# A selective-scan hybrid block on one core: the step's softplus cut into groups, and other places and allowances for the work between the scans

## The chip, the core and the metric

The kernel runs on one core of a Trainium2 chip. The metric is device time in microseconds, the median of the runs. The engines are TensorE (PE; PEld is its weight load), VectorE (DVE), ScalarE (ACT), GpSimd (POOL) and SyncE (SP), whose queue issues all DMAs here.

## What is computed

The input x has 8 images of 64x64 positions and 96 channels, all float32. Two layers follow each other.

```python
# layer 0, on group-normalized x; per image, L = 4096 positions, 192 inner channels, 16 states, 4 directions
xz = x @ in_proj_w.T;  xh, z = split(xz)
xc = silu(conv3x3_depthwise(xh) + conv_b)
xs = [xc[diag], xc[anti], reversed(xc[diag]), reversed(xc[anti])]
dts, Bs, Cs = split(x_proj(xs))
delta = softplus(dt_proj(dts) + bias)
h = h * exp(delta * A) + (delta * u) * B        # a recurrence over the 4096 positions, for each of 16 states
y = sum over states (h * C) + D * u
out = (layernorm(y of the four directions, put back) * ln_w + ln_b) * silu(z) @ out_proj_w.T
x = x + out
# layer 1: linear attention (no softmax) on layernorm(x), then a feed-forward net with values rounded to fp8
```

## The kernel before

**Steps and states.** The recurrence is the core of the work. The diagonal and the antidiagonal order lie in one tile together (2 x 64 partitions by 3 groups of channels), so an image is walked twice: q = 0 forward, q = 1 backward. Each walk is cut into 8 steps of 512 positions, so an image has 16 steps and the program 128. A step m has 16 states n, and the main loop of `run` runs over all 2048 pairs i = 16 m + n. A tile of a step holds 128 partitions x 3 groups x 512 positions.

**What a state takes.** Work of several states is in flight at once; at loop index i:

- ACT makes decay(i+2) = exp(a * delta), three activations of 512 (L923), and, where the state is of kind "A", `times_b(i+2)`: eight activations of 192 that multiply the transposed delta*u by B (feedT, L937).
- VectorE does `recur(i)`: three scans of 512 (L958). The scan reads its feed from one of three PSUM banks. Where the state is of kind "D", VectorE first makes the feed itself with three products (L962) from a row that TensorE has spread (L947).
- TensorE does `turn(i+1)`: for an "A" state, it transposes feedT into the three feed banks (L945), each as soon as the scan of state i has left it. Between these it does `reduce(i-LAG)`: it transposes h of an earlier state into the sum y (L993).
- POOL does `keep(i-1)` (the last column of h as carry for the next step, L974) and `read(i-1)`: h times C (L979).
- SP fetches row C for state i+4 (L914).

The kinds are set by `FEED = "DADADADADADAAAAA"`: six "D" states and ten "A" states to a step. LAG is 4, and h has six buffers, decay three, feedT two.

**The prologue of a step** makes what its states need: rows of dt, B and C (L835, L840, L845, L848), softplus, and delta*u with its transposed copy. The softplus is computed as max(v, 0) + ln(1 + e) with e = exp(-|v|), and a correction for the rounding of 1 + e: ACT does Abs by groups (L860), then one Exp (L862) and one Ln (L865) over all 1536 columns; POOL does two scalar operations (L869, L870) and two products of tiles (L872, L874); VectorE adds max(v, 0) group by group (L879); POOL makes du = delta * u (L886); TensorE and ACT transpose it (L891, L893). The prologue of step m + 2 starts at state 13 of step m.

**Everything else** (the statistics and convolution of the next image: `measures`, `front`; the norms, attention and feed-forward net of the previous image: `tail`) is written as generators. Each yields, ahead of each piece, the engine it is for, a rough cost in us, how many loop indices it must wait (by the table LAGS, or by a number of its own) and whether it needs a PSUM bank; two banks are free for this. The class `Work` hands them out: the main loop calls `work.at(engine, place)` once per index for ACT (between decay and feedT), VectorE (between the second and the third scan) and POOL (after `read`), and three times for TensorE (after each third of turn and reduce). Each call adds an allowance (PLACES: gain and most) to the engine's credit, and pieces are taken while the credit is positive; urgent ones (prologues) may overdraw it. Engines work in the order in which instructions stand, so a piece that waits holds up all behind it on its engine. `work.finish` hands out everything at once until a condition holds; it is called at state 4 + 1 of an image for all that is left (`all_done`), and in `bring` when the next step's input is not there yet.

Of the kernel before, what the change touches and what calls it, by code (L numbers as in the profile page):

```python
# [67 lines left out]
def weights(tc, const, w):  # L68
# [125 lines left out]

LAGS = {
    "AV": (1, 0), "AP": (0, 1), "AG": (0, 0), "VA": (1, 0), "VP": (0, 1), "VG": (0, 0), "PA": (1, 0), "PV": (1, 0),
    "PG": (1, 0), "GA": (1, 0), "GV": (1, 0), "GP": (1, 1), "SA": (3, 0), "SV": (3, 0), "SP": (3, 0), "SG": (3, 0),
# [27 lines left out]
class Work:  # L225
# [4 lines left out]
    PLACES = {"A": (2.0, 2.5), "V": (1.5, 2.0), "G": (3.5, 5.0), "P": (0.85, 1.2), "S": (9.0, 9.0)}  # L230

    def __init__(self, banks):
        self.now = 0
        self.alone = False
        self.urgent, self.jobs, self.streams = [], [], []
        self.free = [(b, -9) for b in banks]
        self.long = []
        self.credit = dict.fromkeys(self.PLACES, 0.0)

    def start(self, gen, urgent=False):  # L240
        j = SimpleNamespace(gen=gen, tag="S", us=0.0, bank=False, spin=False, ready=(self.now, 0), done=False)
        self.proceed(j, None, 0)
        (self.urgent if urgent else self.jobs).append(j)
        return j

    def proceed(self, j, given, place):
# [6 lines left out]
        its, late = LAGS.get(last + tag, (0, 0))  # L253
        if lag is not None:
            its, late = abs(lag), 0
        j.tag, j.us, j.bank, j.spin = tag, us, needs, lag == -1
        j.ready = (self.now + its, 2 if late else 0) if its or late else (self.now, 0)

    def bank_for(self, j, place):
        if j not in self.urgent and not self.alone:  # L260
            if any(u.tag == "P" and u.bank for u in self.urgent) or j.bank == "long" and self.long:
                return None
        for i, (b, when) in enumerate(self.free):
            if when < self.now or place == 2 or self.alone:
# [12 lines left out]
    def at(self, tag, place=0):  # L277
        gain, most = self.PLACES[tag]
        self.credit[tag] = min(most, self.credit[tag] + gain)
        for j in self.urgent + self.jobs:  # L280
            while not j.done and j.tag == tag:
                if j.ready > (self.now, place) and (j.spin or not self.alone):
                    break
                if not self.alone:
                    if self.credit[tag] <= (0.0 if j not in self.urgent else -1.5 if tag == "P" else -99.0):
# [40 lines left out]
    def finish(self, enough):  # L326
# [7 lines left out]
        self.credit = dict.fromkeys(self.PLACES, 0.0)  # L334
# [224 lines left out]
def tail(tc, work, x, out, k, at, b):  # L559
# [3 lines left out]
    with tc.tile_pool(name=f"t1_{b}", bufs=1, **area) as p1:  # L563
# [3 lines left out]
        with tc.tile_pool(name=f"t2_{b}", bufs=2, **area) as p2:  # L567
# [3 lines left out]
            def join(c):  # L571
                s = slice(4 * c, 4 * c + 4)

                def tile(name, shape, bufs=2):
# [11 lines left out]
                while c >= 2 and c - 2 not in joined:  # L586
                    yield SPIN
                gate = tile("gate", [HC, 2, CH])
                nc.sync.dma_start(out=gate, in_=at.gate[:, :, c * CH : (c + 1) * CH])
                st, mv = tile("st", [P, 4, 6]), tile("mv", [P, 4, 2])  # L590
                yn = ys[0]
                for j in range(2):
# [12 lines left out]
                    yield dve(1.0, 0)  # L605
# [3 lines left out]
                    work.release(ps)  # L609
                r, m = yield from rsqrt(nc, p2, k, mv, P, 4, "n")  # L610
# [3 lines left out]
                yg = tile("yg", [HC, 2, CH])  # L614
# [27 lines left out]
                yield dve(1.7, 0)  # L642
# [38 lines left out]
        def attention():  # L681
# [14 lines left out]
            kf = yield from small([DM, DM], "kf", vk, k.w_ff)  # L696
# [11 lines left out]
        with tc.tile_pool(name=f"t3_{b}", bufs=3, **area) as p2:  # L708

            def layers(c):  # L710
# [22 lines left out]
                yield dve(1.7, 0)  # L733
# [48 lines left out]
def run(tc, pool, psum, dram, x, out, w, NB):  # L782
# [37 lines left out]
    def prologue(m):  # L820
# [8 lines left out]
        ps = yield bank(1.0, 0)  # L829
        v = view(ps, P, TB, NX)  # L830
        for j in range(TB):
            if j == 2:
                yield pe(0.8)
# [5 lines left out]
        rows = o.rows = tile("rows", [P, TB, NX])  # L839
# [14 lines left out]

        e = tile("e", [P, G, T], 1)
        for g in range(G):
# [5 lines left out]
        nc.scalar.activation(e, e, AF.Exp, scale=-1.0)  # L862
        yield act(1.5, 1)
        delta = tile("delta", [P, G, T])
        nc.scalar.activation(delta, e, AF.Ln, bias=w.one)  # L865
        duT = tile("duT", [P, TB * G, P])
        f = duT.rearrange("p (g k) t -> p g (k t)", g=G)
        yield gp(3.0)
        nc.gpsimd.tensor_scalar(f, e, 1.0, 1.0, ALU.mult, ALU.add)  # L869
        nc.gpsimd.tensor_scalar(f, f, -1.0, 1.0, ALU.add, ALU.mult)  # L870
        yield gp(3.4, 1)
        nc.gpsimd.tensor_tensor(e, e, f, ALU.subtract)  # L872
        yield gp(3.4, 1)
        nc.gpsimd.tensor_tensor(delta, delta, e, ALU.add)  # L874
        for g in range(G):
# [5 lines left out]
        o.delta = delta  # L881
        yield gp(3.4)
        while m and not made[m - 1].multiplied:
            yield "G", 0.0, -1, False
        du = o.du = tile("du", [P, G, T], 1)
        nc.gpsimd.tensor_tensor(du, delta, u, ALU.mult)  # L886
        for j in range(G):
            ps = yield bank(0.45)
            for i in range(4):
                r, g = divmod(4 * j + i, G)  # L890
                nc.tensor.transpose(ps[:, i * P : (i + 1) * P], du[:, g, r * P : (r + 1) * P], w.ident)  # L891
# [3 lines left out]
        o.duT = duT  # L895

    def bring(m):
# [4 lines left out]
        made[m] = SimpleNamespace(u=u, c={}, multiplied=False)  # L902
# [22 lines left out]
    def times_b(i):  # L925

        m, n = divmod(i, NS)
        o = made[m]
        if FEED[n] == "D":
            return  # L930
# [18 lines left out]
    def recur(i):  # L949
        m, n = divmod(i, NS)  # L950
        _, q, _ = steps[m]
        h = hs[i] = pool.tile([P, G, T], F32, tag="h", name=f"h_{i}", bufs=6)
# [10 lines left out]
        if n == FEED.rindex("D"):  # L963
            made[m].multiplied = True
        scan(0)
        scan(1)
        work.at("V")
# [13 lines left out]
    def reduce(i, part):  # L981
# [15 lines left out]
        if q and n in (1, 2, 3) and part == 2:  # L997
            for j in range(4 * (n - 1), 4 * n):
# [4 lines left out]
                )  # L1003
        if q and n in (8, 9, 10) and part == 2:
# [4 lines left out]
            )  # L1009
        if part == 2:  # L1010
# [35 lines left out]

    def between(b):
# [20 lines left out]
    work.start(prologue(0), urgent=True)  # L1068
    work.finish(lambda: not work.urgent)
# [135 lines left out]
```

## Time and profile before

| what | us |
|---|---|
| median of 3 runs (12140.42 to 12148.66) | 12146.02 |
| the profiled execution | 12157.04 |
| its span | 12155.1 |
| start of the first scan, end of the last | 445.9, 11772.6 |
| POOL busy with L979 | 7073.1 |
| VectorE busy with L958, both forms | 6500.6 + 883.9 |
| ACT busy with decay L923, with feedT L937 | 3976.8, 3670.8 |
| POOL busy with L872, L874, L886 | 441.9, 441.0, 449.4 |
| ACT busy with Exp L862, with Ln L865 | 190.2, 199.9 |
| mean granted TensorE clock | 0.909 of full |

A row of the groups names line, engine, operation, output and inputs with their shapes and the count; then follow the total busy time, the mean of one in ns, and the idle time of the engine just before these instructions with what ended it. A row of the waits names who waited, for whom, the total in us, how often, and the longest. A row of a timeline has start, length, engine, line, operation and count, and in brackets the idle time before it.

### The profile page before, as it was taken

The page shows a single profiled execution, that of the slowest core. Times are in us where ns is not written, and L with a number is a line of the kernel's source. Part 1 is how long each engine was busy: PE and PEld are TensorE (multiplying, and loading weights), DVE is VectorE, ACT ScalarE, POOL GpSimd, SP SyncE. Part 2 cuts the span into 40 slices and gives each one's busy share as a digit, 9 for nine tenths or more (in the row PEclk, how much of TensorE's full clock was granted, in tenths as well). Part 3 has the DMA queues.
Part 4 walks back from the last instruction along what each step waited for, and adds up shares of the span by engine and source line. Part 5 has one row for each costly group of instructions (what it writes and reads, how often), then busy time and mean ns, then how long its engine had stood idle before and what let it go on. Part 6 is the DMA issues. An engine that isn't in the chain of part 4 may idle for free.

```text
span 12155.1 us, 187007 instructions
## 1 busy us (share of the span) xinstructions
PE 9958.7 (82%) x62804; PEld 8012.1 (66%) x62804; DVE 9683.1 (80%) x11092; ACT 9501.2 (78%) x19842; POOL 9737.6 (80%) x6927
## 2 busy tenths in 40 slices
PE   4698889888898888988888888988889888888874
PEld 3476667666676666766677666766667666666653
DVE  1488998878888888888888888888888878888971
ACT  1588888877888788877888878887788878878862
POOL 0588998878988788888888889888898888889972
PEclk9799999998998989989899999999989899988985
DMA  2334333533335433353333433344333443322331
GB/s 53 91 92 124 100 93 94 136 104 96 94 88 134 112 94 93 90 141 101 95 90 106 127 102 95 90 127 117 92 92 93 132 108 93 100 87 84 100 93 42
DMA packets 1138471, 1213.47 MB, mean 100 GB/s; under 512 B 464998, under 2 KB 744167, under 8 KB 1137511
## 3 DMA queue, kind: packets, MB, share of 16 engines
q1 hardware_dynamic: 1137510, 1201.51, 36.0%
q8 instruction: 499, 8.18, 0.3%
q14 instruction: 462, 3.78, 0.1%
HBM read 877.94 MB, written 323.09 MB: 99 GB/s over the span
## 4 chain that ended last, share of the span: by engine, by line
PE 29%; ACT 22%; DVE 20%; POOL 11%; issue 9%; SPq 4%; DMA 4%; DVEq 0%; POOLq 0%; ACTq 0%
DVE h L958 13%; ACT feedT L937 8%; PE y L993 7%; PE feed L945 7%; ACT decay L923 6%; POOL h L979 6%; DVE feed L962 4%; PE bank L493 3%; DMA cc<-crow 2%; PE bank L835 2%; SPq L538 2%; PE bank L877 1%; POOL delta L874 1%; PE feed L947 1%; PE bank L858 1%
## 5 line engine op out<-in xcount | busy, mean ns | idle before, releaser
L979 POOL TENSOR_TENSOR h<-h,cc 128x1536 f32<-128x1536 f32 x2048 | 7073.1, 3454 | 401.7 <-DMA cc<-crow 205.0
L958 DVE TENSOR_TENSOR_SCAN h<-decay,carry,feed 128x512 f32<-128x512 f32 x5376 | 6500.6, 1261 | 623.0 <-PE feed L945 510.4
L923 ACT ACTIVATE decay<-delta,a_neg 128x512 f32<-128x512 f32 x6144 | 3976.8, 713 | 1303.6 <-DVE h L958 1298.1
L945 PE MATMUL feed<-ident,feedT 128*128 128x128 f32 x15360 | 2738.5, 303 | 1508.3 <-DVE h L958 1237.9
L993 PE MATMUL y<-ident,h 128*128 128x128 f32 x24576 | 3804.4, 289 | 68.6 <-ACT ys L1021 37.3
L937 ACT ACTIVATE feedT<-duT,rows 128x192 f32<-128x192 f32 x10240 | 3670.8, 443 | 1.6 <-PE feed L945 1.1
L993 PEld LDWEIGHTS y<-ident,h 128*128 128x128 f32 x24576 | 3154.2, 151 | 527.5 <-issue 483.4
L945 PEld LDWEIGHTS feed<-ident,feedT 128*128 128x128 f32 x15360 | 1970.4, 155 | 2118.5 <-DVE h L958 667.9
L962 DVE TENSOR_TENSOR feed<-feed,du 128x512 f32<-128x512 f32 x2304 | 1442.5, 687 | 210.7 <-PE feed L947 205.8
L974 POOL COPY carry<-h 128x3 f32<-128x3 f32 x2048 | 395.4, 193 | 1065.4 <-DVE h L958 985.8
L958 DVE TENSOR_TENSOR_SCAN h<-decay,feed 128x512 f32<-128x512 f32 x768 | 883.9, 1202 | 102.5 <-PE feed L945 83.2
L493 PE MATMUL bank<-wf,xp 97*128 97x192 f32 x4320 | 873.6, 334 | 1.7 <-ACT xp L458 1.7
L947 PE MATMUL feed<-x,pick 77*128 77x512 f32 x1536 | 846.4, 633 | 0.7
L493 PEld LDWEIGHTS bank<-wf,xp 97*128 97x128 f32 x4320 | 704.8, 195 | 28.8 <-issue 15.9
L879 DVE SCALAR_TENSOR_TENSOR delta<-bank,delta 128x512 f32<-128x512 f32 x381 | 258.5, 678 | 287.0 <-POOL delta L874 159.6
L886 POOL TENSOR_TENSOR du<-delta,u 128x1536 f32<-128x1536 f32 x128 | 449.4, 3511 | 10.6 <-DVE delta L879 10.6
L877 PE MATMUL bank<-x,ws 13*128 13x512 f32 x762 | 439.4, 657 | 20.8 <-DVE delta L879 20.8
L872 POOL TENSOR_TENSOR e<-e,duT 128x1536 f32<-128x1536 f32 x128 | 441.9, 3452 | 16.7 <-ACT delta L865 16.6
L858 PE MATMUL bank<-x,ws 13*128 13x512 f32 x766 | 436.6, 650 | 17.3 <-ACT x L848 17.3
L874 POOL TENSOR_TENSOR delta<-delta,e 128x1536 f32<-128x1536 f32 x128 | 441.0, 3446 | 0.1
L947 PEld LDWEIGHTS feed<-x,pick 77*128 77x128 f32 x1536 | 261.0, 201 | 152.7 <-issue 96.2
L835 PE MATMUL bank<-wx,u 128*128 128x77 f32 x3048 | 356.5, 273 | 0.0
(260 smaller groups left out, 8885.1 us busy)
## 6 DMA issues: line engine op xcount, KB each, us to landing
cc<-crow SPq DMA_DIRECT2D x4096, 128.0 KB
u<-seq SPq DMA_DIRECT2D x256, 384.0 KB
wide<-ys SPq DMA_DIRECT2D x512, 192.0 KB
ut<-image SPq DMA_DIRECT2D x768, 64.0 KB
seq<-us SPq DMA_DIRECT2D x128, 384.0 KB
part<-ys SPq DMA_DIRECT2D x64, 768.0 KB
y<-part SPq DMA_DIRECT2D x64, 768.0 KB
y<-wide SPq DMA_DIRECT2D x256, 192.0 KB
```

The costliest lines, as they stand in the source:

```text
L493: nc.tensor.matmul(v[:, j, :], flat[:, o : o + P], k.wf[:, i, :], start=(i == 0), stop=(i == 8), skip_group_check=True)
L835: nc.tensor.matmul(v[:, j, :], u[:, g, j * P : (j + 1) * P], w.wx[:, q, g, :], start=(g == 0), stop=(g == G - 1))
L874: nc.gpsimd.tensor_tensor(delta, delta, e, ALU.add)
L877: nc.tensor.matmul(ps, w.ws[:, q, g, :], x[0 : 2 * NR + 1, :], start=True, stop=True)
L923: nc.scalar.activation(decays[i][:, g, :], made[m].delta[:, g, :], AF.Exp, scale=w.a_neg[:, q, g, n : n + 1])
L937: nc.scalar.activation(f[part], o.duT[part], AF.Copy, scale=scale)
L945: nc.tensor.transpose(feed[g][:, j * P : (j + 1) * P], feeds[i][:, j * G + g, :], w.ident)
L947: nc.tensor.matmul(feed[0], w.pick[:, FEED[:n].count("D"), :], made[m].x, start=True, stop=True)
L958: nc.vector.tensor_tensor_scan(h[:, g, back], a[:, g, back], feed[g][:, back], init, ALU.mult, ALU.add)
L962: nc.vector.tensor_tensor(feed[g], feed[0], made[m].du[:, g, :], ALU.mult)
L979: nc.gpsimd.tensor_tensor(hs[i], hs[i], c.unsqueeze(1).to_broadcast([P, G, T]), ALU.mult)
L993: nc.tensor.matmul(y[:, j, :], hs[i][:, g, r * P : (r + 1) * P], w.ident, is_transpose=True, start=(n == 0 and j % 4 == 0), stop=(n == NS ...
```

## The change

- **Softplus by groups.** The prologue ends after dt, B and C. It then starts three generators `group(g)`, each with 512 columns: Abs and Exp (one piece), Ln, two scalar operations and two products on POOL, VectorE's correction, and POOL's du. When all three are through, three generators `turned(j)` transpose du. du gets two buffers instead of one, `rows` three instead of two. The groups of step m wait until those of m - 1 are corrected and the last feedT of m - 2 is made. The prologue starts at state 9 instead of 13, and its first matmuls come in four pieces instead of two.
- **Allowances by kind.** Each engine has two gains, one for a "D" and one for an "A" state: ACT 1.45 and 0.3 (for state i + 2), VectorE 0.3 and 1.9, TensorE 1.0 and 0.9, POOL 2.0 and 2.0. Urgent pieces may overdraw only to -1.0 (ACT) or -0.4. TensorE's extra matmuls of `reduce` are counted as spent.
- **Places.** VectorE's place is behind the third scan, after TensorE's. ACT has a second place at the end of the index, behind feedT. LAGS names the place at which the piece before was handed out.
- **Ends may run over.** The fronts and tails of all images are one stream, `windows`, which may go on into the next image's steps; the `finish` at an image's start is gone. `hurry` hands out urgent pieces at once where the next decay or feedT needs them.
- **Buffers.** LAG is 3 instead of 4, h has five buffers instead of six, the tail's first pool has three instead of two (gate and yg stay at two). In `join`, the wait for c - 2 and the fetch of gate come after the first sums; its and `layers`' bn_stats take their lag from LAGS.
- **Start.** The prologues of steps 0 and 1 are handed out together before the loop.

```diff
-    PLACES = {"A": (2.0, 2.5), "V": (1.5, 2.0), "G": (3.5, 5.0), "P": (0.85, 1.2), "S": (9.0, 9.0)}
+    GAIN = {"A": (1.45, 0.3), "V": (0.3, 1.9), "G": (2.0, 2.0), "P": (1.0, 0.9), "S": (9.0, 9.0)}
+    MOST = {"A": 3.2, "V": 2.2, "G": 2.5, "P": 1.2, "S": 9.0}
...
-    def at(self, tag, place=0):
-        gain, most = self.PLACES[tag]
-        self.credit[tag] = min(most, self.credit[tag] + gain)
-        for j in self.urgent + self.jobs:
+    def at(self, tag, place=0, kind="D"):
+        self.credit[tag] = min(self.MOST[tag], self.credit[tag] + self.GAIN[tag][kind != "D"])
+        for j in self.urgent + ([] if self.hurried else self.jobs):
...
-                    if self.credit[tag] <= (0.0 if j not in self.urgent else -1.5 if tag == "P" else -99.0):
+                    if self.credit[tag] <= (0.0 if j not in self.urgent else -1.0 if tag == "A" else -0.4):
...
-        for g in range(G):
-            ps = yield bank(0.85)
-            nc.tensor.matmul(ps, w.ws[:, q, g, :], x[0 : 2 * NR + 1, :], start=True, stop=True)
-            yield act(0.6)
-            nc.scalar.activation(e[:, g, :], ps, AF.Abs)
-            work.release(ps)
-        nc.scalar.activation(e, e, AF.Exp, scale=-1.0)
-        yield act(1.5, 1)
-        delta = tile("delta", [P, G, T])
-        nc.scalar.activation(delta, e, AF.Ln, bias=w.one)
...
+        def group(g):
+
+            ps = yield bank(0.85)
+            nc.tensor.matmul(ps, w.ws[:, q, g, :], x[0 : 2 * NR + 1, :], start=True, stop=True)
+            yield act(0.6)
+            nc.scalar.activation(e[:, g, :], ps, AF.Abs)
+            work.release(ps)
+            nc.scalar.activation(e[:, g, :], e[:, g, :], AF.Exp, scale=-1.0)
+            yield act(1.2)
+            nc.scalar.activation(delta[:, g, :], e[:, g, :], AF.Ln, bias=w.one)
+            yield gp(1.05)
+            nc.gpsimd.tensor_scalar(f[:, g], e[:, g], 1.0, 1.0, ALU.mult, ALU.add)
+            nc.gpsimd.tensor_scalar(f[:, g], f[:, g], -1.0, 1.0, ALU.add, ALU.mult)
+            yield gp(1.15)
+            nc.gpsimd.tensor_tensor(e[:, g], e[:, g], f[:, g], ALU.subtract)
+            yield gp(1.15)
+            nc.gpsimd.tensor_tensor(delta[:, g], delta[:, g], e[:, g], ALU.add)
+            ps = yield bank(0.85)
+            nc.tensor.matmul(ps, w.ws[:, q, g, :], x[0 : 2 * NR + 1, :], start=True, stop=True)
+            yield dve(0.7)
+            nc.vector.scalar_tensor_tensor(delta[:, g, :], ps, 0.0, delta[:, g, :], ALU.max, ALU.add)
+            work.release(ps)
...
+            yield gp(1.15)
+            nc.gpsimd.tensor_tensor(o.du[:, g], delta[:, g], u[:, g], ALU.mult)
...
-        h = hs[i] = pool.tile([P, G, T], F32, tag="h", name=f"h_{i}", bufs=6)
+        h = hs[i] = pool.tile([P, G, T], F32, tag="h", name=f"h_{i}", bufs=5)
...
         scan(0)
         scan(1)
-        work.at("V")
         scan(2)
...
-    LAG = 4
+    LAG = 3
...
             if at == LAG + 1:
-                work.finish(all_done)
-                work.stream(between(b))
+                begun[0] = b
+                if b == 0:
+                    work.stream(windows())
...
         if i + 2 < total:
+            work.hurry(lambda: made[(i + 2) // NS].corrected)
             decay(i + 2)
-        work.at("A")
+        work.at("A", 0, FEED[(i + 2) % NS])
         if i + 2 < total:
+            if FEED[(i + 2) % NS] == "A":
+                work.hurry(lambda: hasattr(made[(i + 2) // NS], "duT"))
             times_b(i + 2)
         if i < total:
             recur(i)
-        else:
-            work.at("V")
         for part in range(3):
             if i + 1 < total:
                 turn(i + 1, part)
             if 0 <= i - LAG < total:
                 reduce(i - LAG, part)
-            work.at("P", part)
+            work.at("P", part, FEED[(i + 1) % NS])
+        work.at("V", 0, FEED[n])
+        work.at("A", 1, FEED[(i + 2) % NS])
```

## The prediction

> **What bounds the kernel now.** I read the page first: busy shares, then the costliest groups. (Mean durations of ACT, VectorE and TensorE overlap the next instruction, so below I price repeats by their pitch, start to start in the trace: scan 1.171 us, feed product 0.596, decay 0.612, feedT 0.345, POOL's read 3.40 and carry 0.265.)
>
> ```profile
> PE 9958.7 (82%) x62804; PEld 8012.1 (66%) x62804; DVE 9683.1 (80%) x11092; ACT 9501.2 (78%) x19842; POOL 9737.6 (80%) x6927
> ...
> L979 POOL TENSOR_TENSOR h<-h,cc 128x1536 f32<-128x1536 f32 x2048 | 7073.1, 3454 | 401.7 <-DMA cc<-crow 205.0
> L958 DVE TENSOR_TENSOR_SCAN h<-decay,carry,feed 128x512 f32<-128x512 f32 x5376 | 6500.6, 1261 | 623.0 <-PE feed L945 510.4
> ...
> L872 POOL TENSOR_TENSOR e<-e,duT 128x1536 f32<-128x1536 f32 x128 | 441.9, 3452 | 16.7 <-ACT delta L865 16.6
> ```
>
> Four engines at 78 to 82% and none full: the loss is in their meeting. The first scan starts at 446 us, the last ends at 11773: 2048 states in 11327 us, 88.5 us for each step of 16 states, then a tail of 382. All 128 steps do the same scans, so I compared steps of one image with the windows view (columns: window, length, busy us and instructions by engine, TensorE clock, DMA share, GB/s). Step 2 is the second row, step 3 the third, step 8 the fourth:
>
> ```profile
> 4634.00:4713.00 79.00, 61.23 (x394) 47.87 (x393) 68.56 (x70) 68.09 (x145) 70.64 (x41) 0.91 0.28 73
> 4801.00:4892.00 91.00, 79.74 (x498) 65.20 (x497) 74.13 (x76) 75.69 (x148) 70.58 (x36) 0.94 0.30 88
> 4893.00:4974.00 81.00, 78.10 (x531) 65.05 (x530) 74.88 (x77) 72.81 (x145) 70.54 (x36) 1.00 0.30 89
> 5324.00:5426.00 102.00, 84.92 (x544) 71.12 (x543) 78.13 (x112) 75.01 (x164) 80.79 (x82) 0.90 0.29 88
> ```
>
> Steps 2 and 3 are equally loaded on VectorE (74.1 and 74.9), ACT and POOL, and take 92.3 and 81.4 us (means of six images; each within 0.3). So what a job costs depends on where it stands. The timelines of ACT and then of VectorE in step 2, at its state 15, show how:
>
> ```profile
> 4878.51 1.28 ACT L509 ACT_TABLE_LOAD   x1
> 4879.80 0.85 ACT L509 ACTIVATE pre<-pre 128x768 f32<-128x768 f32 x1
> 4880.55 1.04 ACT L510 ACTIVATE z<-z 96x1024 f32<-96x1024 f32 x1
> 4881.61 1.28 ACT L64 ACT_TABLE_LOAD   x1
> 4882.91 2.87 ACT L937 ACTIVATE feedT<-duT,rows 128x192 f32<-128x192 f32 x8
> ```
>
> ```profile
> 4880.75 1.28 DVE L958 TENSOR_TENSOR_SCAN h<-decay,carry,feed 128x512 f32<-128x512 f32 x1 [0.57 <-PE feed L945]
> 4886.27 1.28 DVE L958 TENSOR_TENSOR_SCAN h<-decay,carry,feed 128x512 f32<-128x512 f32 x1 [4.24 <-PE feed L945]
> ```
>
> The convolution's two Silus and their table loads (4.4 us) stand between decay and feedT of an "A" state; the transposes, then the scan, wait 4.24 us. The waits view has the other kind, jobs that VectorE meets too early, between its second and third scan:
>
> ```profile
> DVE h L958 <- PE feed L945: 593.6, 468, 4.7
> DVE st L607 <- ACT y L604: 244.1, 91, 23.5
> DVE feed L962 <- PE feed L947: 205.8, 243, 11.2
> ...
> DVE st L735 <- ACT t L731: 190.4, 50, 26.1
> ...
> DVE delta L879 <- POOL delta L874: 187.3, 30, 27.7
> ```
>
> **The change, part by part.** I summed, state by state, the order of the built programs' instructions times those pitches (states of the middle steps; the number of a state is n):
>
> *Softplus by groups.* POOL's five instructions per step become fifteen. No 512-wide POOL product is in the trace; L979 at 1536 (3454 ns) and L776 at 384 (914) give 2.2 ns an element and 67 ns fixed, so 10 more instructions cost 0.67 us a step, 86 us of POOL time. On ACT, Exp and Ln (1.39 and 1.47 us pitch) become six. A rule speaks against it: the Trainium skill, Perfetto Trace Analysis, section Optimizing Scalar/DVE Operations, puts about 93 ns on each ScalarE instruction with its data in SBUF and advises larger operations where the engine is saturated. By it, four more cost 0.37 us a step (48 us in all); by the nearest row, decay's 0.612, 6 x 0.612 - 2.86 = 0.81 (104 us). No 512-wide Exp without a scale operand is in the trace, so the row is the upper end; I take about 0.6. At state 0, a "D" state, VectorE's 5.6 us cover it; uncovered, 104 us come back. In return 3.4-us blocks vanish: POOL's states 3, 4, 5 held 6.2, 7.0 and 7.8 us; now states 1 to 8 hold 6.8, 5.9, 5.9, 5.3, 5.8, 5.3, 5.5, 4.7. VectorE's correction has a state between it and POOL, so of L879's wait for POOL (187 us, 1.5 a step) I count all as gone; POOL's backlog, below, is what is late next.
>
> *ACT's second place and allowances by kind.* Before, 42 of the 56 Silu blocks inside the loop stand between decay and feedT of an "A" state; after, 3 do; 29 come after feedT, and 24 at "D" states, where ACT has 1.84 us of own work against VectorE's 5.3. The pair of steps above prices a whole step of such placing: 92.3 against 81.4. But the second place makes ACT wait for a TensorE job of the same state: behind that wait stands the next decay, which waits for the scan anyway (L923 idles 1298 us for it now), so zero at "D" states, at most 1 us at "A" ones.
>
> *VectorE's place after the third scan.* ACT's copy is then older by a scan (1.2 us) or more; the bn_stats waits (L607, L735, L644: 581 us, some 360 of it inside the loop, 2.8 a step) should fall to a third, 0.9. Queued behind a late job now are the next state's scans instead of the third scan; the feed banks get filled meanwhile.
>
> *Ends run over.* Tails spread: VectorE's load per step, 69 to 79 us over the 16 steps of an image before, is 72 to 76 after; POOL's 72 to 87 becomes 73 to 82. But the allowances are smaller than the work: in images 4 to 6 the front is not ready when its first tile is fetched, and the rest of it (12, 20 and 12 us of TensorE work, with a Silu block, DRAM round trip and transposes in line) stands in one state. Bounds for each: 0 (it is work that had to be done) and 50 us; I take 25, so 75. And five of the eight last-layer chunks of image 6 fall behind the loop: the present tail does eight in 159 us (223 to 382), so 5/8 x 159 = 99, less the 17 us it now waits for its first load: 80.
>
> *h kept in five buffers instead of six, read by TensorE three states later instead of four:* no work, but POOL's allowed lateness falls. POOL must have read h when TensorE gets to it: two states and a scan, about 11.3 us, less its own 3.66, so 7.5 us; before about 12. Prelude: both pipelines there shift by some us each way; zero.
>
> **The sum for a step.** VectorE's own work after: 73.0 us (73.2 before). States 9 to 13: ACT has 26.4 us, VectorE 20.4; feedT can be some 2.1 us late (two states, 7.4, less a transpose 0.7 and 4.6 of ACT's own), so 3.9 remain. POOL in states 0 to 8: 49.8 against VectorE's 44.7, a backlog of 5.1 to 6.4 within the 7.5: I take 1.5. Waits for the "D" feed (206 us / 128 = 1.6): 1.3. bn_stats 0.9. Other job waits, as now, 1.2; unexplained scan waits 1.2. Sum 83.0. Check: step 3, the one with its Silus at "D" states, has 81.4 at 73 of VectorE and 5 us less POOL.
>
> 446 + 128 x 83.0 (10624) + 75 + (382 + 80) = 11607, and 2 us around the span: 11609 against the profiled 12157. The median of the runs is 11 us under that execution: **11600 us**, 4.5% faster.
>
> **Rivals.**
> 1. *POOL's lateness becomes the bound (slower).* In states 1 to 5 POOL gets 29.7 us of work while VectorE has 23.3: 6.4 us late, 1.1 below the limit of the shortened path. If lateness passes 7.5 us by state 5, TensorE waits at L993 with the next transposes behind it, VectorE with it; the step is then POOL's 49.8, plus 28.3 + 3.9, plus step 3's other waits in full (81.4 - 73 = 8.4): 90.4. 446 + 11571 + 75 + 462 = 12554, and 12545 as a median. For it: POOL at 80%, more instructions. Against: step 0, with the highest POOL load in the first row relative to VectorE, takes 79 us. Chance 0.15.
> 2. *Only the front's half gains.* If "A" states with join jobs stay as dear, half of the steps keep 88: mean 85.5, 446 + 10944 + 75 + 462 = 11927, median 11920. For it: step 8's many small chained jobs (x112 on VectorE). Chance 0.20.
> 3. *The lags absorb both backlogs:* 80 a step, dumps 40, tail 430: 446 + 10240 + 40 + 430 = 11156, median 11150. Against: ACT's 26.4 in the "A" run. Chance 0.15.
> 4. *It gives all back* (87.3 a step): within 0.2% of now. Chance 0.03.
> The forecast (11350 to 11800) has 0.47. A measurement here cannot tell less than about 0.2% from no change. Faster 0.47 + 0.20 + 0.15 = 0.82, same 0.03, slower 0.15. The range, 11150 to 12100, leaves out rival 1 and the far end of rival 3.
>
> **What would show it.** After: scans' wait for PE feed well under 594 us, st's waits under 250 in all, L879 waiting for POOL hardly at all; a step some 83 us with steps 2 and 8 no longer apart; three gaps of 15 to 50 us near state 7 of an image's step 14; a tail near 460. Wrong: PE's y transposes (L993 before) waiting hundreds of us for POOL's h (rival 1); join steps still near 100 (rival 2).

## The result, and the profile after

The changed kernel takes 13382.78 us (median of 4 runs, 13364.52 to 13392.49) against 12143.22 for the kernel before (4 runs, 12137.30 to 12148.66): ratio 1.1019, 95% interval 1.1000 to 1.1038. It is 10% slower; forecast was 4.5% faster. The profiled execution took 13386.89 us with a span of 13385.1. Its first scan starts at 453 us (before: 446), the last ends at 12934, so the loop takes 12481 us (11327), 97.5 us for each step of 16 states (88.5), and the tail 451 (382).

The page of the changed kernel: the busy shares, and the groups of VectorE's scans, TensorE's transposes of h, POOL's product du and VectorE's correction:

```profile
PE 10549.4 (79%) x62804; PEld 8411.9 (63%) x62804; DVE 9766.9 (73%) x11092; ACT 9607.1 (72%) x20354; POOL 9965.7 (74%) x8207
...
L1000 DVE TENSOR_TENSOR_SCAN h<-decay,carry,feed 128x512 f32<-128x512 f32 x5376 | 6526.6, 1263 | 1266.0 <-PE feed L987 1057.4
...
L1032 PE MATMUL y<-ident,h 128*128 128x128 f32 x24576 | 4057.0, 297 | 40.1 <-ACT ys L1062 21.6
...
L917 POOL TENSOR_TENSOR du<-delta,u 128x512 f32<-128x512 f32 x384 | 497.5, 1296 | 684.5 <-DVE delta L911 658.0
...
L911 DVE SCALAR_TENSOR_TENSOR delta<-bank,delta 128x512 f32<-128x512 f32 x383 | 264.7, 691 | 807.4 <-PE bank L909 743.6
```

The rows of TensorE's transposes of h and of the correction in the kernel before:

```profile
L993 PE MATMUL y<-ident,h 128*128 128x128 f32 x24576 | 3804.4, 289 | 68.6 <-ACT ys L1021 37.3
...
L879 DVE SCALAR_TENSOR_TENSOR delta<-bank,delta 128x512 f32<-128x512 f32 x381 | 258.5, 678 | 287.0 <-POOL delta L874 159.6
```

All four engines have lost share, since their work grew by less than the span: VectorE is busy 84 us more, ScalarE 106, POOL 228 and TensorE, with as many matmuls, 591, while the span has 1230 more. The scans' idle time ahead of them has doubled. The correction, 265 us of work, has 807 us of idle time ahead of it (287 before), and POOL's product behind it 685. TensorE's transposes of h have 40 us ahead of them (69 before), so rival 1 did not come true in the form it was given. The waits view of the changed kernel (who waits, for whom, us in all, times, longest):

```profile
DVE h L1000 <- PE feed L987: 1200.9, 811, 33.0
...
DVE delta L911 <- PE bank L909: 743.6, 353, 8.5
POOL du L917 <- DVE delta L911: 658.0, 224, 10.1
ACT rows L867 <- PE bank L862: 592.3, 102, 26.0
...
PE bank L862 <- DMA u<-seq: 225.4, 46, 22.0
...
DVE st L762 <- ACT t L758: 137.6, 24, 24.6
...
DVE st L630 <- ACT y L627: 88.4, 18, 26.2
```

The second row is the finding: of 384 corrections, 353 wait for the matmul that they read. Before, 125 did, for 122 us in all:

```profile
DVE delta L879 <- PE bank L877: 121.6, 125, 2.4
```

In the view of the changed kernel, the fourth and fifth rows are another new wait: TensorE stands for u's DMA, and ScalarE behind TensorE. The last two rows, with L671's 51.1, make 277 us of waits at bn_stats, 581 before; nearly all that is left lies outside the loop. That step came out about as forecast (under 250 in all). The timelines of VectorE and then of TensorE around one correction:

```profile
5539.52 3.62 DVE L1000 TENSOR_TENSOR_SCAN h<-decay,carry,feed 128x512 f32<-128x512 f32 x3
5544.28 0.69 DVE L911 SCALAR_TENSOR_TENSOR delta<-bank,delta 128x512 f32<-128x512 f32 x1 [1.14 <-PE bank L909]
5544.89 3.62 DVE L1000 TENSOR_TENSOR_SCAN h<-decay,carry,feed 128x512 f32<-128x512 f32 x3
```

```profile
5542.03 0.66 PE L987 MATMUL feed<-ident,feedT 128*128 128x128 f32 x4
5542.52 0.60 PE L1032 MATMUL y<-ident,h 128*128 128x128 f32 x4
5543.05 1.12 PE L909 MATMUL bank<-x,ws 13*128 13x512 f32 x2
```

VectorE has its three scans done at 5543.14 and meets the correction. Its matmul was put into the same state, behind the transposes for two of the next state's three feed banks, and began at 5543.05. VectorE stands 1.14 us. The next scan could not start before the correction was through, although its own feed had long been there. Wait and correction together put 1.75 us between two scans.

To see where a step's time went, I added up VectorE's idle time (gaps over 0.12 us, states 40 to 2039, so 125 steps) by the instruction behind the gap. In us a step, with the prediction's terms in the same classes, and two later runs:

| VectorE idle ahead of | before | predicted | after | run 9, mended | run 14, before with ScalarE's second place |
|---|---|---|---|---|---|
| scans | 5.4 | 6.6 | 10.9 | 9.4 | 7.3 |
| feed products, "D" states | 1.5 | 1.3 | 0.7 | 1.1 | 1.4 |
| correction | 2.2 | 0 | 6.3 | 1.4 | 1.8 |
| bn_stats | 2.9 | 0.9 | 0.2 | 0.9 | 1.4 |
| other foreign work | 1.2 | 1.2 | 3.6 | 1.3 | 0.9 |
| sum | 13.2 | 10.0 | 21.7 | 14.1 | 12.8 |

The predicted sum needs care: the prediction counted VectorE's own work by pitch, 73.0 us a step (73.2 before). In these steps of the traces VectorE is busy 75.4 us (74.9 before). So the 10.0 goes with 88.5 - 73.2 = 15.3 for the kernel before, and not with 13.2.

### The profile page after: what moved, and what is told of

Same layout as the page of the kernel before. It is cut to its first block, busy times and chain, and to the rows that moved or that the text cites. A ratio compares the mean times of both kernels' runs of the same rounds, so it can differ in the third digit from the quotient of the medians.

```text
span 13385.1 us, 189394 instructions
## 1 busy us (share of the span) xinstructions
PE 10549.4 (79%) x62804; PEld 8411.9 (63%) x62804; DVE 9766.9 (73%) x11092; ACT 9607.1 (72%) x20354; POOL 9965.7 (74%) x8207
## 5 line engine op out<-in xcount | busy, mean ns | idle before, releaser
L987 PE MATMUL feed<-ident,feedT 128*128 128x128 f32 x15360 | 2921.6, 311 | 1719.8 <-DVE h L1000 1271.5
L1032 PE MATMUL y<-ident,h 128*128 128x128 f32 x24576 | 4057.0, 297 | 40.1 <-ACT ys L1062 21.6
L1032 PEld LDWEIGHTS y<-ident,h 128*128 128x128 f32 x24576 | 3299.2, 157 | 661.2 <-issue 522.7
L987 PEld LDWEIGHTS feed<-ident,feedT 128*128 128x128 f32 x15360 | 2082.3, 159 | 2572.4 <-issue 946.9
L917 POOL TENSOR_TENSOR du<-delta,u 128x512 f32<-128x512 f32 x384 | 497.5, 1296 | 684.5 <-DVE delta L911 658.0
L911 DVE SCALAR_TENSOR_TENSOR delta<-bank,delta 128x512 f32<-128x512 f32 x383 | 264.7, 691 | 807.4 <-PE bank L909 743.6
L862 PE MATMUL bank<-wx,u 128*128 128x77 f32 x3024 | 430.6, 299 | 225.6 <-DMA u<-seq 225.4
L862 PEld LDWEIGHTS bank<-wx,u 128*128 128x128 f32 x3024 | 415.4, 218 | 236.0 <-issue 227.6
L894 PE MATMUL bank<-x,ws 13*128 13x512 f32 x762 | 549.1, 835 | 0.0
L907 POOL TENSOR_TENSOR delta<-delta,e 128x512 f32<-128x512 f32 x384 | 491.4, 1280 | 17.6
L905 POOL TENSOR_TENSOR e<-e,duT 128x512 f32<-128x512 f32 x384 | 488.6, 1272 | 21.2
```

The lines of the kernel that those rows point to most:

```text
L862: nc.tensor.matmul(v[:, j, :], u[:, g, j * P : (j + 1) * P], w.wx[:, q, g, :], start=(g == 0), stop=(g == G - 1))
L894: nc.tensor.matmul(ps, w.ws[:, q, g, :], x[0 : 2 * NR + 1, :], start=True, stop=True)
L917: nc.gpsimd.tensor_tensor(o.du[:, g], delta[:, g], u[:, g], ALU.mult)
L987: nc.tensor.transpose(feed[g][:, j * P : (j + 1) * P], feeds[i][:, j * G + g, :], w.ident)
L1032: nc.tensor.matmul(y[:, j, :], hs[i][:, g, r * P : (r + 1) * P], w.ident, is_transpose=True, start=(n == 0 and j % 4 == 0), stop=(n == NS ...
```

## The experiments

My first theory: VectorE now meets foreign work in the same state in which TensorE produces it, and stands. That comes of two lines of the change together: VectorE's place moved behind TensorE's places of the same index, and LAGS lets VectorE take a TensorE result at once ("P0V" and "P1V" are (0, 0), where "PV" was (1, 0); the first number says how many loop indices the next piece must wait, the second from which place on). Rivals: the many small pieces; ScalarE's second place; the earlier prologue; TensorE's clock, granted at 0.858 of full in place of 0.909. All ratios below are to the kernel before, measured beside it.

**Run 1: the correction alone gets the lag back.**

```diff
-            yield dve(0.7)
+            yield dve(0.7, 1)
             nc.vector.scalar_tensor_tensor(delta[:, g, :], ps, 0.0, delta[:, g, :], ALU.max, ALU.add)
```

> The changed kernel, with one lag: the group's correction on VectorE may be placed one state after its matmul at the earliest, not in the same state. First theory (the loss is the chain TensorE matmul, VectorE correction, POOL product inside one state): VectorE's wait in front of L911 falls from 744 us to under 150, POOL's in front of L917 from 658 to under 300, and the time falls by about what VectorE gains, 400 to 700 us, to 12700-13000. Rival (these waits stand where VectorE would have waited for the next state's feed anyway): the waits at L911 go, but the scans wait that much longer for TensorE, and the time stays within 150 us of 13383.

13191.34 us (1.0850, 1.0834 to 1.0866): 191 less than the changed kernel, a third of what I expected. The idle time at L911 did fall, from 787 to 24 us of the tally above. But each correction comes a state later, so the foreign work as a whole is slower, and more of it is left over: the long states near an image's end add up to 427 us in eight states (changed kernel: 208 in six), about 206 more than usual states would, and the tail is 535 (451). Without these 290 the gain would be 480, if the left-over work cost nothing elsewhere; run 2 speaks against that. VectorE also waits longer ahead of other foreign work, 580 us of the tally in place of 400. So the wait is real, and its removal was partly paid back as left-over work and as other waits.

**Runs 2 and 3: allowances.** Run 2 raises TensorE's gain and ceiling ("P" below), run 3 all of them. The edit of run 3:

```diff
-    GAIN = {"A": (1.45, 0.3), "V": (0.3, 1.9), "G": (2.0, 2.0), "P": (1.0, 0.9), "S": (9.0, 9.0)}
-    MOST = {"A": 3.2, "V": 2.2, "G": 2.5, "P": 1.2, "S": 9.0}
+    GAIN = {"A": (1.8, 0.6), "V": (1.0, 2.0), "G": (2.6, 2.6), "P": (1.3, 1.2), "S": (9.0, 9.0)}
+    MOST = {"A": 3.6, "V": 2.4, "G": 3.4, "P": 1.6, "S": 9.0}
```

> The changed kernel with TensorE's allowance raised from 1.0/0.9 to 1.3/1.2 us a state (and its ceiling from 1.2 to 1.6), all else as it is: no work is left over at an image's end, so the three gaps of 50 to 75 us near an image's last step and the tail's 69 us more go. If these are additive: 13383 - 3 x 55 - 69 = about 13150. If larger pieces of foreign work on TensorE between its feeds cost as much as the gaps did: 13300 or more. The waits at L911 should stay near 744 us either way.

> The changed kernel with all allowances raised (ScalarE 1.8/0.6, VectorE 1.0/2.0, TensorE 1.3/1.2, POOL 2.6, and the ceilings with them): no left-over work, as with TensorE's alone. It is the base that the next kernel is compared with. If the allowances by the state's kind matter by themselves (work put into the wrong kind of state), it is 200 us or more slower than the kernel with TensorE's alone raised; if not, within 100 us of it. First theory: 13000-13250, waits at L911 still over 500 us.

13418.86 (1.1034) and 13430.49 (1.1043): 36 and 48 us above the changed kernel, hardly more than the intervals can tell, and not faster, although the gaps at the image ends and the long tail are gone (tails 396 and 390). The median step rose instead, from 95.6 to 97.2 us in run 2. What stood in the gaps is work that has to be done, and it costs as much between the scans. The sizes of the allowances carry none of the loss.

**Run 4: VectorE's place back, on the base of run 3.**

```diff
-    "P0A": (0, 1), "P0V": (0, 0), "P0G": (1, 0), "P1A": (0, 1), "P1V": (0, 0), "P1G": (1, 0),
+    "P0A": (0, 1), "P0V": (1, 0), "P0G": (1, 0), "P1A": (0, 1), "P1V": (1, 0), "P1G": (1, 0),
...
         scan(1)
+        work.at("V", 0, FEED[n])
         scan(2)
...
-        work.at("V", 0, FEED[n])
         work.at("A", 1, FEED[(i + 2) % NS])
```

> As the kernel with all allowances raised, but VectorE's place is back between the second and third scan, and VectorE follows TensorE's jobs by one state again, as before the change. Softplus by groups, ScalarE's second place, the later prologue, the allowances by kind and the ends that run over all stay. First theory (VectorE's place and its same-state wait carry most of the loss): at least 500 us below the kernel with all allowances raised, at 12200-12600, waits at L911 under 150 us. Rival (pieces, ScalarE's second place and the prologue at state 9 carry the loss): within 200 us of it.

12675.61 (1.0429, 1.0413 to 1.0445): 755 us less than run 3, as the first theory had it, though just above its range; the idle time at L911 falls from 865 to 52.

**Run 6: the converse, in the kernel before.** VectorE's place moves behind TensorE's and "PV" becomes (0, 0); nothing else.

> The kernel before, with one part of the change alone: VectorE's place for foreign work moved from between the second and third scan to the iteration's end, behind TensorE's places, with no lag from TensorE to VectorE. First theory (this place carries most of the loss, whatever the pieces): 12650-12950, of which up to 150 is a gap at each image's start, since VectorE's jobs come later and are finished there; waits of VectorE at its correction (L879) and at the jobs' bank reads rise to several hundred us. Rival (the place costs only together with softplus in pieces): under 12400.

13393.69 (1.1019, 1.1001 to 1.1038): this one edit makes the kernel before as slow as the whole change did. That is more than expected. In this kernel foreign work must be finished at an image's start, and since it comes later, six states there take 74 to 76 us each: about 6 x 68 = 410 us. The other 830 are near run 4's 755. The groups of VectorE in run 6 show the same row as the changed kernel, with softplus undivided:

```profile
L879 DVE SCALAR_TENSOR_TENSOR delta<-bank,delta 128x512 f32<-128x512 f32 x381 | 263.6, 692 | 819.0 <-PE bank L877 714.6 <-POOL delta L874 58.8 <-POOL h L978 24.1
```

**Run 11: place or lag?** Run 3 with "P0V" and "P1V" at (1, 0), VectorE's place left at the end.

> The changed kernel with all allowances raised (13430), VectorE's place left at the iteration's end, but all of VectorE's jobs may follow TensorE's only one state later. It parts the lag from the place: the kernel with the place in the middle and the same lag took 12676. If the same-state wait is the whole loss: about 12700, plus up to 150 for work left over at three image ends. If the place itself is (nothing of VectorE's own lies between the job and the next state's scans, so its length and its wait go straight into the period): 13200 or more.

12842.79 (1.0574, 1.0559 to 1.0590), 588 less than run 3, and VectorE's groups lose the wait:

```profile
L1000 DVE TENSOR_TENSOR_SCAN h<-decay,carry,feed 128x512 f32<-128x512 f32 x5376 | 6544.0, 1264 | 1575.2 <-PE feed L987 1342.5 <-ACT t L667 31.7 <-ACT feedT L979 22.4
...
L911 DVE SCALAR_TENSOR_TENSOR delta<-bank,delta 128x512 f32<-128x512 f32 x383 | 254.9, 666 | 19.9 <-POOL delta L907 15.3 <-PE bank L909 4.6
```

Its loop takes 11802 us, run 4's 11818, and its tail 587 us against 391. The loops are alike in sum only: run 11 has seven long states with left-over work near the image ends (396 us together), run 4 has twelve of 26 to 33 us of another kind (359 us; run 5 looks at them). So reading TensorE's results in the same state is most of the loss. That the place at the end costs nothing by itself is not shown so exactly; with a lag it makes the chain of foreign work longer, and the ends pay for it.

**Run 5: the prologue at state 11 in place of 9**, on the base of run 4; **run 9: at 13**, as before the change.

```diff
-            if n == 9 and m + 2 < len(steps):
+            if n == 11 and m + 2 < len(steps):
                 work.start(prologue(m + 2), urgent=m + 2)
             if n == 8 and m + 2 < len(steps):
                 bring(m + 2)
```

> The kernel with VectorE's place back in the middle (12676), with the prologue of the next step but one started at state 11 in place of 9, so three states after the DMA that brings its u in place of one. First theory: what is left of the loss is mostly TensorE standing in front of L862 for u's DMA (333 us of waits and 324 more put down to issue there, ScalarE's 600 at L867 behind them, scans waiting up to 27.6 us): those fall to a third, and the time to 12250-12450. Rival (ScalarE's second place and the pieces themselves carry the rest): the waits go, but the time stays within 100 us of 12676.

> The kernel with VectorE's place back in the middle, with the prologue started at state 13 (before the change: 13, after: 9), so five states after the order for u's DMA. In the run with 11, u's two DMAs were issued up to 25 us late, behind a burst of 36 DMA orders (ut, L565: 24.1 us) on SyncE's queue, and 14 states with TensorE standing at L862 for it took 25 to 32 us in place of 5. First theory: these 14 gaps go (14 x 22 = 308 us): 12427 - 308 = about 12120, between 12050 and 12200. Rival (the later prologue leaves too few states to the softplus pieces, and the next step's decays wait): 12350 or more.

Run 5: 12427.11 (1.0225, 1.0210 to 1.0240), 249 less than run 4. That is in the expected range, but not for the reason given. TensorE's idle time ahead of L862 that the trace puts down to u's DMA or to issue fell only from 658 to 574 us, not to a third, and 14 states take 25 to 32 us, where run 4 had its twelve. The other states got cheaper; why was not tried. The timelines of SyncE (DMA orders) and then of TensorE in run 5 show one:

```profile
862.06 24.10 SPq L565 DMA_DIRECT2D ut<-image  x36
886.26 1.20 SPq L955 DMA_DIRECT2D cc<-crow  x2
887.50 1.26 SPq L945 DMA_DIRECT2D u<-seq  x2
```

```profile
870.95 0.60 PE L1033 MATMUL y<-ident,h 128*128 128x128 f32 x4
895.39 4.12 PE L862 MATMUL bank<-wx,u 128*128 128x77 f32 x18 [23.85 <-DMA u<-seq]
```

The order for u stands behind 36 orders of a foreign job, which keep SyncE busy for 24.1 us. TensorE has meanwhile come to the first matmul that reads u, and everything behind that matmul stands 23.85 us. With the prologue at 13 TensorE idles 8 us ahead of L862, no state is over 22 us any more, and run 9 takes 12326.25 (1.0143, 1.0127 to 1.0160). That is 101 less than run 5, not 308: the other states got dearer.

**Run 10: ScalarE also one state behind TensorE** ("P0A" and "P1A" at (1, 0) in run 9).

> As the kernel with VectorE's place in the middle and the prologue at 13, but ScalarE follows TensorE's jobs by one state (before: one state as well; changed kernel: same state, at the second place). First theory (a same-state wait costs on ScalarE as it did on VectorE, only less, because ScalarE's second place stands behind the state's own work): 50 to 150 us faster than with the same-state lag. Rival (ScalarE's second place hides it): within 50 us, or slower, since every job takes one state more.

12752.98 (1.0496, 1.0480 to 1.0511): 427 slower, so my expectation was wrong in sign, and the rival had it. For ScalarE the same-state wait at the second place is cheap, as the prediction had said, and on this base the lag is dear (in the kernel before, run 14 below, the second place without a lag makes no difference).

**Run 7: softplus in pieces, alone in the kernel before.** Exp, Ln and POOL's instructions are issued as three of 512 columns, at the old places.

> The kernel before, with one part of the change alone: softplus's Exp, Ln and POOL's instructions are issued as three of 512 columns in place of one of 1536, at the same places and with the same grants. First theory: the shorter instructions' fixed costs (POOL 10 more a step, ScalarE 4 more, on engines that are not the last to arrive) cost little: 12143 to 12300. Rival (many short instructions are the loss): 12500 or more.

12203.95 (1.0042, 1.0027 to 1.0057): 49 us. The pieces are not the loss.

**Runs 8, 12 and 13: TensorE's clock.** Zero matmuls are added to the changed kernel, to run 9 and to the kernel before: four in each of six states of a step (in the kernel before in five, because the condition below leaves one out at its LAG of 4).

```diff
+        if 0 <= i - LAG < total and (i - LAG) % NS != NS - 1 and FEED[(i + 1) % NS] == "D":
+            for j in range(4):
+                nc.tensor.matmul(sums[(i - LAG) // NS][:, j, :], w.ident, zero.to_broadcast([P, P]), start=False, stop=False, skip_group_check=True)
```

> The changed kernel with four matmuls of zeros (128x128, added to the running y, so that the result stays) behind TensorE's last place in each state whose successor takes its feed by the pick matmul: 24 a step, about 0.3 us each, 7 us a step of TensorE's time where it mostly waits for VectorE. First theory (TensorE's half-speed stretches follow from the waits and are not their cause): half-speed time falls by less than a third, and the time stays within 200 us of 13383 or rises. Rival (the granted clock is the cause: TensorE falls idle a little more often, the clock is halved, all gets longer): half-speed time falls from 3.8 ms to under 2.5 ms, and the time by over 300 us.

> The kernel with VectorE's place in the middle and the prologue at 13 (12326), with four matmuls of zeros behind TensorE's last place in each state whose successor takes its feed by the pick matmul. On the changed kernel these cut the loop's half-speed time from 3267 to 2305 us and the time by 124 us. If the clock carries the rest of the loss against the kernel before (170 us): half-speed time from 2380 to under 1800 and 12150-12250. If it doesn't: half-speed time falls, and the time stays within 50 us of 12326 or rises, since they cost 7 us a step of TensorE's time.

> The kernel before with the same matmuls of zeros. If the clock sets a part of its time too: 12000-12100. If TensorE at half speed only follows waits that would be there anyway: 12150-12350.

| kernel | half-speed time in the loop, us | with zero matmuls | time, us | with zero matmuls |
|---|---|---|---|---|
| changed | 3267 | 2305 | 13382.78 | 13259.02 (1.0909) |
| run 9 | 2381 | 1518 | 12326.25 | 12295.15 (1.0127) |
| before | 1771 | 1287 | 12151.94 | 12176.45 (1.0023) |

Half-speed time is the time in which the clock granted to TensorE was half of full. More work on TensorE goes with less of it: the mean granted clock rises from 0.858 to 0.893 in the changed kernel, from 0.884 to 0.919 in run 9, from 0.909 to 0.928 in the kernel before. The row of the zeros in run 8, where each is recorded as two matmuls:

```profile
L1175 PE MATMUL y<-zero,ident 128*128 128x128 f32 x6144 | 840.8, 280 | 0.0
```

The Trainium skill (TensorE: Matmul & The Clock Gate, Part 1: The HAM clock gate) says that half speed is TensorE's default, and that sustained work releases it. The half-speed column agrees. By the page's price (section Terms: penalty about the throttled time times one minus the granted share) the 962 us taken off the changed kernel would be worth an estimated 480; the run gained 124, and the kernel before lost 25. Both are net of what the zeros themselves cost, which no run parts from them. TensorE's other matmuls give a second measure: they are busy 10549 us in the changed kernel, 10173 with the zeros, 9959 before. So 376 of the 591 us that they had grown by came back, but only 124 of the 1240 us of time. I take it that most of the half-speed time lies in stretches in which TensorE waits anyway: it follows from the waits and adds some to them. It is not the main cause; its exact share stays open.

**Run 14: ScalarE's second place, alone in the kernel before.** "PA" becomes (0, 1), ScalarE's gain 1.0 at each place.

```diff
             work.at("P", part)
+        work.at("A", 2)
```

> The kernel before with one part of the change alone: a second place for ScalarE's foreign work at the iteration's end, with no lag behind TensorE's jobs there, and ScalarE's allowance halved for each of the two places. The prediction counted this part as a gain (foreign Silu and copies no longer between a decay and the feedT of the same state): 11950-12100. Rival (the feedT or the decay of the next state wait instead, since ScalarE now stands in front of TensorE's last job): 12200-12400.

12151.15 (1.0004, 0.9995 to 1.0013): no change, so neither theory's range holds it. The table of idle time has the reason: bn_stats and the correction wait 1.9 us a step less, the scans 1.9 more. The groups of VectorE in run 14:

```profile
L958 DVE TENSOR_TENSOR_SCAN h<-decay,carry,feed 128x512 f32<-128x512 f32 x5376 | 6530.8, 1263 | 857.7 <-PE feed L945 610.9 <-ACT rows L840 58.0 <-ACT feedT L937 57.9
...
L607 DVE BATCH_NORM_STATS2 st<-bank 128x6 f32<-128x192 f32 x238 | 81.6, 343 | 138.2 <-ACT y L604 137.8
...
L735 DVE BATCH_NORM_STATS2 st<-bank 128x6 f32<-128x96 f32 x240 | 57.3, 239 | 126.6 <-ACT t L731 126.0
```

**Run 15: is VectorE's sum the path?** In the kernel before, the line of the correction (L879) is taken out.

> The kernel before, with VectorE's correction of softplus (L879, 384 instructions) left out; the matmul that it reads is still made, and delta stays without that term, so the output is another. In the profile of before these took 259 us and 287 us of idle time ahead of them: 546 us of VectorE. If VectorE's busy time and waits add up to the period, as the prediction's sum had it: 11600-11750. If the loop of feed and scan is the bound, and VectorE's idle time only moves: a third of it or less, 11970-12150.

11985.51 (0.9868, 0.9851 to 0.9884): 164 us of the 546, 30%. Ahead of scans and feed products the tally shows 251 us more idle time than before (1109 against 858).

**Run 16: the shorter path of h, alone in the kernel before.** LAG 3, five buffers of h.

> The kernel before with one part of the change alone: LAG 3 in place of 4 and five buffers of h in place of six, the start of an image's joining work kept at the same state. If POOL's shortened lateness (7.5 us in place of 12, rival 1 of the prediction) costs: 12220-12300, with TensorE's y transposes (L993) waiting for POOL's h. If not: within 30 us of 12150.

12374.19 (1.0192, 1.0175 to 1.0209): 221 us slower. Its waits:

```profile
ACT ys L1021 <- PE y L993: 177.6, 53, 5.9
...
ACT ys L1026 <- PE y L993: 144.2, 56, 9.7
...
PEld y L993 <- POOL h L979: 110.9, 105, 3.7
...
PE y L993 <- POOL h L979: 57.8, 37, 3.5
```

TensorE does wait for POOL's h at L993, as rival 1 feared (58 us of matmuls and 111 of weight loads, which may overlap; 4 and 18 before). A second wait is one that nobody had named: ScalarE's copy of y at the end of a step (L1021, L1026), which stands 322 us for TensorE's last transposes, 41 before. How much of the 221 us comes of each was not parted. The copy falls one state earlier now, behind the transposes for an "A" state in place of a "D" state's one matmul; that TensorE comes to y later for this reason is inferred from the order, not tried.

## Why the prediction was wrong

**The step that failed** is the one on VectorE's place: "Queued behind a late job now are the next state's scans instead of the third scan; the feed banks get filled meanwhile." I had seen who is queued, and priced it at nothing, because I took the late jobs to be ScalarE's copies, which are older at the new place. That half held: bn_stats went to 0.2 us a step (forecast 0.9). For TensorE's results it is the other way round. The place stands behind TensorE's places of the same index, and the lag is nil, so the matmul is fresh, and it stands in TensorE's queue behind transposes that wait for the scans. I had weighed just this for ScalarE ("the second place makes ACT wait for a TensorE job of the same state") and not for VectorE, whose two entries changed in the same table. Of the correction I looked only at its wait for POOL (187 us, "all as gone"; it is 65) and not at the one for TensorE (122 us, now 744). Shown by runs 4 and 11 (755 and 588 us, two ways of putting the lag back) and run 6 (the edit alone gives all of the loss, 410 us of it at the image starts).

**A moved step's DMA.** The prologue was moved from state 13 to 9, right behind the order for its u. I counted what it issues, and not what it reads: its first matmul depends on a DMA ordered one state before. Putting it back to 13 is worth 349 us (runs 4 and 9). The timeline shows one of its costs, the wait behind SyncE's burst, but the time does not follow it: from 9 to 11 TensorE's idle time ahead of L862 hardly fell and the time fell by 249 us; from 11 to 13 that idle time went and the time fell by 101. So what carries the 349 stays open in the main.

**The sum was not a sum.** With both mended, run 9 has 89.7 us a step, not 83.0: 4.1 of the difference is idle time (14.1 against 10.0), and 2.2 is own work counted too small (75.2 busy in the trace, 73.0 by pitch). The prediction took VectorE's own work plus its waits as the path, so that a wait taken away shortens the step. Run 14 took away 1.9 us a step of foreign waits and got 1.9 us of scan waits; run 15 took away 546 us and got 164. In these two runs VectorE's idle time mostly moved to another place. Not every wait is so: putting the lag back took 813 us off the correction's wait and 755 off the time in run 4, 852 and 588 in run 11. My check of the sum, step 3 at 81.4 us against step 2 at 92.3, compared two steps of one kernel in which everything else was equal too; it does not say what one edit brings.

**Rival 1 had the right part, and half of the mechanism at most.** In the changed kernel TensorE's y transposes wait almost nothing; ScalarE's copies of y wait 178 us for them (41 before). The shorter path of h does cost, 221 us by itself in the kernel before, where both waits appear. Run 9 lies 174 us above before; the pieces (49) and this path are in it. Their prices alone come to 270, so something of the change gives back about 100, or they overlap; which one stays open. Run 9 with LAG 4 and six buffers of h was not tried.

**What came right:** the prelude (453, forecast 446) and the tail (451, forecast 462); the length of POOL's pieces (1.27 to 1.30 us, 1.19 by the two rows) and their low price; ScalarE's 0.6 us a step for the pieces of Exp and Ln (in run 7 their pitches are 0.54 and 0.61 us, so 3 x 1.15 - 2.86 = 0.59, between the prediction's two estimates, 0.37 by the page it cites and 0.81 by decay's row); ScalarE's second place harmless; three gaps at the named places. The gaps' size was off: 208 us in six states, about 170 more than usual ones, where 75 was taken. Run 2 showed that they aren't a cost of their own.

No version here that does the whole work beats the kernel before. The nearest of the changed ones is run 9 with zero matmuls (12295); run 14 equals it.

## What to carry to other kernels

Where a schedule moves an engine's place for foreign work, go through all pairs of engines: whose result does it meet there, how old is that result, and what of its own work stands behind the wait. Reading TensorE's result in the same state was free for one engine (ScalarE, runs 10 and 14) and cost 588 to 755 us for another (VectorE, runs 4 and 11). In a loop whose engines are all near 80% busy, do not add up one engine's waits; take one wait away in a run and see how much of it arrives. Here it was nothing in run 14, a quarter to a third in runs 1 and 15, and over two thirds in runs 4 and 11.

## What the runs showed of the hardware that I had not expected

- In run 5 SyncE gave 36 DMA orders of one job in 24.1 us, 0.67 us each, and the order for u behind them started that much later: how late this load was issued depended on the burst ahead of it in the queue.
- 3072 matmuls of zeros, 841 us of TensorE's busy time, made the changed kernel 124 us faster (run 8); 2560 of them made the kernel before only 25 slower (run 13).
